# A four-layer graph network: layer 2 in written order, and inverse roots by ScalarE and a Newton step

## The chip, the cores and the metric

The kernel runs on one core of a Trainium2 chip. Its engines work side by side, each through its own queue of instructions: TensorE (PE in the profile, with its weight loads as PEld), VectorE (DVE), ScalarE (ACT), GpSimd (POOL) and SyncE (SP), which issues most DMAs. The metric is the device time of one execution in microseconds (us). One execution was also recorded by the hardware profiler; lines such as L941 are lines of the kernel before.

## The reference

16 graphs ("batches") share one adjacency matrix of 1024 x 1024; every node has 64 features. Four layers follow one another, each of them `x = layernorm(x + layer(x, adj))`:

```python
def gat(x, W, a, adj):                      # layers 0 and 2
    Wh = x @ W
    e = leaky_relu((Wh @ a1)[:, :, None] + (Wh @ a2)[:, None, :], 0.2)
    att = softmax(where(adj > 0, e, -big), axis=2)
    return elu(att @ Wh)

def softmax_average(x, w0, b0, wa, ba, adj):  # layer 1
    feat = softplus(x * w0 / sqrt(2) + b0)
    logits = where(adj > 0, feat * wa + ba, -big)   # one weight per feature
    return sum_j softmax_j(logits) * feat_j

def layer_3(x, adj, Wh, Wo, ...):             # four heads, then one output head
    z = leaky_relu(concat(attention(h, h, adj | eye) for each head), 0.2)
    return layernorm(leaky_relu(attention(z @ Wo, z @ Wo, adj | eye), 0.2)) * gamma + beta

def layernorm(x):
    return (x - mean(x)) / sqrt(var(x) + 1e-5)
```

`a1` and `a2` are the halves of `a`. The layer norm needs one inverse root of `var + eps` for each of 16 x 1024 nodes in every layer. How that inverse root is computed is half of the change.

## The kernel before

Everything stays in on-chip memory between the layers. The nodes are cut into C = 8 chunks of 128 partitions, and x lies in four tiles `xg[g]` of four batches each. `fast_path` (L579) is the program that runs; a general path is there for inputs that the fast path's flags reject.

**Layers 0 and 2** are one function, `gat_layer` (L862), called twice. A pair of batches is prepared in a chain: `prep_x` transposes x by PE into PSUM and ACT copies it to `xT` (L880, L881); `prep_s` makes the scores (PE `ps`, L886); `prep_top` copies them on DVE (`l_s`, L894), takes the maximum (L896) and gives it to GpSimd for a maximum over the partitions (`gtop`, L898); `prep_p` makes the factors `p` and `q` by two Exps on ACT (L909, L911); `prep_G` multiplies on PE (`pg`, L921) and takes an Exp on ACT (`G`, L922), in two halves; `prep_v` scales x by `p` on ACT (`vals`, L928).

Then each batch is eight units, one for a chunk of nodes. `unit(k)` is one DVE instruction over 128 x 1024, `e = max(G, q) * adjacency` (L941); `product(k, e)` two PE matmuls with `vals` as weights (`y`, L953), two units later (LAG = 2). In layer 0 PE also makes the row sums by separate matmuls (`u`, L964); in layer 2 a column of ones in `vals` gives them (`zero_mean`). When a batch's units are through, its tail runs in these steps: `evict` (ACT copies y, L971), `project` (PE, L983 and L987), `divide` (DVE L996 to L1001, ACT Exp `m` L1008), `residual` (DVE L1013, L1014), `norm` (DVE `bn_stats` L1021, and for every second batch `moments`), `shift` (DVE `bn_shift`) and `store` (ACT `scaled`, eight activations that write x).

The steps are put in slots (t, k): batch number and unit number. `slots` holds the list, and the loop over t and k calls a unit, a product and the slot's steps in turn. In both layers this is the order of the program; the order on each engine is however chosen by a planner that reorders instructions by cost and priority, since the loop doesn't run in a manual schedule. Layer 3 does: it is under `tc.manual_schedule(engines=in_order)`, in which PE, ACT, DVE and GpSimd keep the order as written.

**The inverse root.** `moments` (L733) works on a pair of batches (128 x 16 values) in layers 0 and 2 and on a group of four batches (128 x 32) in layer 1. DVE combines the statistics (L739 to L745), GpSimd raises the variance to the power −0.5 and DVE makes the shift from the result when the returned function is called:

```python
nc.gpsimd.tensor_tensor(t["rstd"], t["var"], neg_half[:, :n], ALU.pow)
def finish():
    v.scalar_tensor_tensor(t["shift"], t["mean"], -0.5, t["rstd"], ALU.mult, ALU.mult)
    return t["rstd"], t["shift"]
```

ACT's `scaled` (L758) then applies root and shift. Layer 3 already has another way (L718 to L726): ACT takes a Ln and an Exp with scale −0.5, and DVE one Newton step. Only its last batches use the power (L712, "late"). `most_var` keeps the largest variance seen, which one of the flags at the end is made from (L714). A list `soon` holds tasks that are called at the next `catch_up()`, in layer 3 alone.

**Layer 1** goes through the four groups g. `prep_l1` prepares the next group (transposes L1462, softplus by ACT's Abs, Exp, Relu and Ln L1464 to L1468, exponents L1476 to L1481, transposes L1490, split in two halves L1492 and L1493) while `product_l1` (L1507, 16 matmuls per chunk) and `average` (DVE L1516 to L1522) work on this one. The group's `shift` and four `rows` (eight activations each) are done beside the next group, and those of the last group in layer 2's first slots. In the same way the last steps of layer 0 run in layer 1 and those of layer 2 in layer 3 (`ending`).

Of the kernel before, what the change touches and what calls it, by code (L numbers as in the profile page):

```python
# [578 lines left out]
def fast_path(  # L579
# [66 lines left out]
    nc.vector.memset(ones, 1.0)  # L646
    neg_half = const.tile([P, GB * C], F32, tag="neg_half", name="neg_half")
    nc.vector.memset(neg_half, -0.5)
    most_var = const.tile([P, C], F32, tag="most_var", name="most_var")
    nc.vector.memset(most_var, 0.0)  # L650
# [14 lines left out]

    rings = {}
    soon = []

    def two_banks(name):
# [15 lines left out]
    def bc_mid(ap, n):  # L685

        return ap.unsqueeze(1).to_broadcast([P, n, ap.shape[1]])

    def normalizing(y, sq, late):

        n, t = y.shape[1], {}

        def mean():
            st = small.tile([P, n], F32, tag="ln_sum", name="ln_sum")
            nc.vector.tensor_reduce(st, y, AX.X, ALU.add)
            t["mean"] = small.tile([P, n], F32, tag="ln_mean", name="ln_mean")
            nc.vector.tensor_scalar(t["mean"], st, 1.0 / D, None, ALU.mult)

        def centre():
            nc.vector.tensor_tensor(y, y, bc_last(t["mean"], D), ALU.subtract)
            nc.vector.tensor_tensor(sq, y, y, ALU.mult)

        def scale():
            vs = small.tile([P, n], F32, tag="ln_vs", name="ln_vs")
            nc.vector.tensor_reduce(vs, sq, AX.X, ALU.add)
            ve = small.tile([P, n], F32, tag="ln_ve", name="ln_ve")
            nc.vector.tensor_scalar(ve, vs, 1.0 / D, LN_EPS, ALU.mult, ALU.add)
            rstd = small.tile([P, n], F32, tag="ln_rstd", name="ln_rstd")  # L710
            if late:
                nc.gpsimd.tensor_tensor(rstd, ve, neg_half[:, :n], ALU.pow)  # L712
                return rstd
            nc.vector.tensor_tensor(most_var[:, :n], most_var[:, :n], ve, ALU.max)  # L714


            def first():
                nc.scalar.activation(rstd, ve, AF.Ln)  # L718
                nc.scalar.activation(rstd, rstd, AF.Exp, scale=-0.5)
                soon.append(step)  # L720

            def step():
                t = small.tile([P, n], F32, tag="ln_step", name="ln_step", bufs=1)
                nc.vector.scalar_tensor_tensor(t, rstd, -0.5, rstd, ALU.mult, ALU.mult)
                nc.vector.tensor_tensor(t, t, ve, ALU.mult)
                nc.vector.scalar_tensor_tensor(rstd, t, 1.5, rstd, ALU.add, ALU.mult)  # L726

            soon.append(first)
            return rstd

        return mean, centre, scale

    def moments(st):  # L733


        n = st.shape[1]
        t = {k: small.tile([P, n], F32, tag=f"bn_{k}", name=f"bn_{k}") for k in ("mean", "d", "var", "rstd", "shift")}
        v = nc.vector
# [6 lines left out]
        v.tensor_tensor(t["var"], t["var"], t["d"], ALU.add)  # L745
        nc.gpsimd.tensor_tensor(t["rstd"], t["var"], neg_half[:, :n], ALU.pow)  # L746

        def finish():
            v.scalar_tensor_tensor(t["shift"], t["mean"], -0.5, t["rstd"], ALU.mult, ALU.mult)  # L749
            return t["rstd"], t["shift"]  # L750

        return finish

# [107 lines left out]

    def gat_layer(w, name, zero_mean, extra, first, own):  # L862

        w1, w4, ind, s12, sums, w_out = (w[k] for k in ("w1", "w4", "ind", "s12", "sums", "out"))
        F = D - 1 if zero_mean else D
# [68 lines left out]
        def attention(b):  # L936
# [73 lines left out]
            def residual():  # L1010

                v, m = held["v"], held["m"]
                nc.vector.scalar_tensor_tensor(v, v, 0.0, xb(b), ALU.max, ALU.add)  # L1013
                nc.vector.scalar_tensor_tensor(m, m, 1.0, v, ALU.min, ALU.add)  # L1014
            def norm():
                pair = stats.setdefault(b // 2, {})
# [5 lines left out]
                if b % 2:  # L1022
                    pair["end"] = moments(st)

            def shift():
                if b % 2:
                    stats[b // 2]["n"] = stats[b // 2]["end"]()

# [3 lines left out]

            return unit, product, [evict, project, divide, residual, norm, shift, store]

# [9 lines left out]
        for b in range(B):  # L1044
            end = (3, 6) if b % 2 == 0 else (3, 2)
            for task, (t, k) in zip(work[b][2], ((1, 1), (1, 2), (1, 4), (1, 6), (1, 7), (2, 1), end)):
                at(b + t, k, task)
# [12 lines left out]
        for (t, k), todo in extra.items():  # L1060
            for task in todo:
                at(t, k, task)
        first(ahead)
        for t in range(B + 1):
            for k in range(C):
                if t < B:
                    unit, product, _ = work[t]
# [4 lines left out]
                if t < B or (t == B and k < own):  # L1072
                    for task in slots.get((t, k), []):
                        task()

        return [task for t in range(B, B + 3) for k in range(C) for task in slots.get((t, k), []) if (t, k) >= (B, own)]
# [75 lines left out]
    def shift_of(key, sq):  # L1152
# [17 lines left out]

        if "s" in rings:
            soon.append(below)
        else:
            below()

# [236 lines left out]
    with tc.tile_pool(name="ps_g", bufs=1, space=bass.MemoryType.PSUM, reuse_waits="tile") as ps_g, tc.tile_pool(  # L1412
# [18 lines left out]
        extra = {(0, 6): [lambda: gat_setup(later["w2"], "l2", True)], (1, 6): [lambda: later["w3"]()]}  # L1431
        ending = gat_layer(w_0, "l0", False, extra, first, 3)

# [13 lines left out]
    with tc.tile_pool(name="l1", bufs=2, reuse_waits="tile") as l1, tc.tile_pool(  # L1447
# [66 lines left out]
        def average(g, ic, po, st):  # L1514
            r = l1.tile([P, 2, P], F32, tag="r1", name="r1")
            nc.vector.reciprocal(r, po[:, :, 1, :])  # L1516
# [11 lines left out]
        for g in range(NG):  # L1528
# [9 lines left out]

            def shift(mo=mo, end=moments(st)):
                mo["n"] = end()  # L1540
# [3 lines left out]

            last = [shift] + [lambda c=c, rows=rows: rows(c) for c in range(C * GB // 8)]

# [65 lines left out]
    with tc.tile_pool(name="ps_g", bufs=1, space=bass.MemoryType.PSUM, reuse_waits="tile") as ps_g, tc.tile_pool(  # L1612
# [3 lines left out]
        extra = {p: [task] for p, task in zip(places, ahead)}  # L1616
        for p, task in zip(((0, 1), (0, 3), (0, 7), (1, 3), (1, 7)), last):
            extra.setdefault(p, []).append(task)
# [4 lines left out]

        ending = gat_layer(later["w2"], "l2", True, extra, first, 5)
    for p, task in zip((2, 4, 8, 10, 13), ending):
        at(0, p, task)
# [13 lines left out]

    def catch_up():
        for task in [soon.pop(0) for _ in range(len(soon))]:
            task()

    def tasks(where, b, j):
# [10 lines left out]
    last = [(E, LAST + p, unit) for p, unit in enumerate(outs[E][1][0])]  # L1656


    in_order = {getattr(mybir.EngineType, e) for e in ("PE", "Activation", "DVE", "Pool")}

# [99 lines left out]
```

## Time and profile before

| | |
|---|---|
| Runs | 2199.07, 2201.24 and 2202.79 us; median 2201.24 |
| Profiled execution | 2202.97 us |
| Its span (first to last instruction) | 2201.1 us |
| Mean clock of TensorE, as a share of full speed | 0.971 |
| ACT busy | 1223.3 us (56%) |
| Stretches of the trace | layer 0 from 34 us, layer 1's first product at 337, layer 2's first unit at 514, layer 3 from 754 to the end |

The span leaves out what lies around the first and last instruction, 1.9 us here. A group in the profile names the line, the engine, the operation and its tiles (output <- inputs) with their shapes; "x20 | 71.9, 3596" means 20 instructions, 71.9 us busy, 3596 ns each on average; what follows is the idle time just before them and what ended most of it. A wait is written as "engine tile line <- engine tile line": who waited for whom, with the total in us, the count and the longest. Waits overlap with work on other engines, so they can't be summed over engines.

### The profile page before, as it was taken

To read this page: it belongs to the slowest core of one execution; us is meant where nothing else is said; L and a number is where in the kernel's file an instruction comes from. 1 tells how busy PE (TensorE), PEld (TensorE's weight loads), DVE (VectorE), ACT (ScalarE), POOL (GpSimd) and SP (SyncE) were. 2 spreads that over 40 slices of the span, in tenths; PEclk is the share of its full clock that TensorE was granted. 3 is DMA by queue.
4 is the path that set the end of the run, shared out by engine and by line. 5 is a ranking of instruction groups with operands and counts; after the bars stand their busy time and mean duration, and the time that the engine had idled before them with its cause. 6 is when DMAs were issued, how large, how long until landed. Compare 5 with 4: busy or idle time off the path is not lost.

```text
span 2201.1 us, 26623 instructions
## 1 busy us (share of the span) xinstructions
PE 2061.3 (94%) x10321; PEld 871.2 (40%) x10321; DVE 1835.6 (83%) x3141; ACT 1223.3 (56%) x1925; POOL 125.5 (6%) x97
## 2 busy tenths in 40 slices
PE   7999979897889899999999999999999999999993
PEld 3333337673334333433333333333333333333331
DVE  5877877886878886788889888889889889888997
ACT  4444544735544566655655665655665665565551
POOL 0010110011110100000000000000000000000001
PEclk9999989997999899999999999999999999999996
DMA  6000000000000010000000000000000000000000
GB/s 160 1 1 1 1 1 1 1 1 1 1 1 1 29 48 1 1 1 6 1 6 1 6 6 1 6 6 1 6 1 6 6 1 6 6 1 6 1 5 16
DMA packets 23655, 18.92 MB, mean 9 GB/s; under 512 B 19361, under 2 KB 19426, under 8 KB 23522
## 3 DMA queue, kind: packets, MB, share of 16 engines
q1 hardware_dynamic: 23218, 17.11, 2.7%
q8 instruction: 83, 1.36, 0.3%
q14 instruction: 50, 0.41, 0.1%
q10 hardware_dynamic: 304, 0.03, 0.0%
HBM read 12.95 MB, written 4.19 MB: 8 GB/s over the span
## 4 chain that ended last, share of the span: by engine, by line
PE 74%; DVE 18%; ACT 3%; POOL 2%; issue 1%; DMA 0%; SPq 0%; POOLq 0%; DVEq 0%; ACTq 0%
PE y L1235 18%; PE s L1223 17%; PE y_l L953 9%; PE s L1320 5%; PE y L1347 4%; DVE e L1228 4%; PE u_l L964 3%; DVE e L941 3%; PE po L1507 3%; PE po L1252 3%; POOL bn_rstd L746 2%; PE pg L921 2%; ACT e L1227 1%; PE ps L886 1%; PE po L987 1%
## 5 line engine op out<-in xcount | busy, mean ns | idle before, releaser
L1227 ACT ACTIVATE e<-s,shift 128x1024 f32<-128x1024 f32 x512 | 543.1, 1112 | 244.8 <-PE s L1223 239.2
L1228 DVE TENSOR_TENSOR e<-e,aT 128x1024 f32<-128x1024 f32 x512 | 602.6, 1220 | 86.8 <-ACT e L1227 84.7
L1223 PE MATMUL s<-hT 64*128 64x512 f32 x2048 | 509.9, 612 | 14.5 <-DVE top L1161 7.6
L1235 PE MATMUL y<-e,vals 128*64 128x512 f32 x2048 | 490.6, 601 | 3.4 <-ACT yT L1242 1.6
L941 DVE SCALAR_TENSOR_TENSOR e<-G_l,q,aT 128x1024 f32<-128x1024 f32 x256 | 319.0, 1273 | 11.2 <-ACT G_l L922 4.2
L953 PE MATMUL y_l<-e,vals_l 128*64 128x512 f32 x1024 | 273.4, 631 | 20.8 <-DVE e L941 20.7
L1223 PEld LDWEIGHTS s<-hT 64*128 64x128 f32 x2048 | 182.6, 186 | 254.7 <-issue 170.2
L1235 PEld LDWEIGHTS y<-e,vals 128*64 128x64 f32 x2048 | 131.0, 136 | 330.7 <-issue 258.8
L1325 ACT ACTIVATE e<-s,shift 128x1024 f32<-128x1024 f32 x128 | 142.1, 1113 | 85.5 <-PE s L1320 75.8
L1327 DVE TENSOR_TENSOR me<-e,aT 128x1024 f32<-128x1024 f32 x128 | 155.9, 1220 | 17.3 <-ACT e L1325 17.0
L1338 DVE SCALAR_TENSOR_TENSOR junk<-e,aN 128x1024 bf16<-128x1024 f32 x128 | 155.9, 1218 | 0.2
L1347 PE MATMUL y<-me,h2v 128*64 128x512 f32 x512 | 135.0, 608 | 10.0 <-DVE me L1327 9.8
L1320 PE MATMUL s<-h2T 64*128 64x512 f32 x512 | 137.4, 617 | 4.5 <-DVE h2v L1307 4.4
L953 PEld LDWEIGHTS y_l<-e,vals_l 128*64 128x64 f32 x1024 | 62.6, 139 | 167.0 <-issue 75.3
L1507 PE MATMUL po<-hi,aR 128*128 128x512 f32 x256 | 105.3, 411 | 13.1 <-DVE r L1517 11.9
L758 ACT ACTIVATE x<-m,bn_shift,bn_rstd 128x64 f32<-128x64 f32 x256 | 90.6, 430 | 32.2 <-DVE bn_shift L749 32.2
L1163 POOL PARTITION_ALL_REDUCE gtop<-top x48 | 28.1, 589 | 1355.5 <-DVE top L1161 852.1
L1507 PE MATMUL po<-lo,aR 128*128 128x512 f32 x256 | 103.3, 404 | 0.0
L746 POOL TENSOR_TENSOR bn_rstd<-bn_var,neg_half 128x16 f32<-128x16 f32 (+1 forms) x20 | 71.9, 3596 | 329.4 <-DVE bn_var L745 166.6
L964 PE MATMUL u_l<-e,only 128*32 128x512 f32 x512 | 78.7, 612 | 0.0
L1282 ACT COPY zT<-pzT 128x1024 f32<-128x1024 f32 x32 | 32.4, 1012 | 78.4 <-PE pzT L1281 78.4
L1252 PEld LDWEIGHTS po<-wb,yT 128*128 128x128 f32 x512 | 62.0, 190 | 34.0 <-issue 21.1
(209 smaller groups left out, 2108.6 us busy)
## 6 DMA issues: line engine op xcount, KB each, us to landing
adj<-in_adj_dram SPq DMA_DIRECT2D x16, 512.0 KB, 4.6
x<-in_x_dram SPq DMA_DIRECT2D x16, 256.0 KB, 5.1
out_dram<-res SPq DMA_DIRECT2D x16, 256.0 KB, 2.0
wl<-in_L_gnn_Wh_dram SPq DMA_DIRECT2D x2, 64.0 KB, 3.2
wo<-in_L_gnn_Wo_dram SPq DMA_DIRECT2D x1, 64.0 KB, 2.8
l_wd<-in_L_gnn_W_dram ACTq DMA_DIRECT2D x2, 16.0 KB, 3.9
l_wd<-in_L_gnn_W_dram SPq DMA_DIRECT2D x2, 16.0 KB, 2.0
bo<-in_L_gnn_bo_dram SPq DMA_DIRECT2D x1, 32.0 KB, 3.0
```

The lines of the kernel that those rows point to most:

```text
L941: nc.vector.scalar_tensor_tensor(e, G[b - b % 2][:, b % 2, :], pq[b - b % 2][1][:, k, b % 2 : b % 2 + 1], aT[:, k, :], ALU.max, ALU.mult,)
L953: nc.tensor.matmul(held["y"][h * D : (h + 1) * D, :], vals[b][:, k, :], e[:, h * HALF : (h + 1) * HALF], start=(k == 0), stop=(k == C - 1),)
L964: nc.tensor.matmul(held["t"][r * 32 : (r + 1) * 32, :], only[b][:, kk, :], ee[:, h * HALF : (h + 1) * HALF], start=(kk < 2), stop=(kk >= C ...
L1223: nc.tensor.matmul(s[:, i, :], hT[rows, k * P : (k + 1) * P], hT[rows, cols], start=True, stop=True)
L1227: nc.scalar.activation(e, s, AF.Exp, bias=shifts[b, n])
L1228: nc.vector.tensor_tensor(e, e, bc_mid(aT[:, k, cols], 2), ALU.mult)
L1235: nc.tensor.matmul(held[h][i * D : (i + 1) * D, :], vals[b][:, k, :], e[:, i, :], start=(k == 0), stop=(k == C - 1),)
L1320: nc.tensor.matmul(s[:, i, :], hT[rows, (i + k // CH) % 2, k % CH * P : (k % CH + 1) * P], hT[rows, 0, :], start=True, stop=True,)
L1327: nc.vector.tensor_tensor(m, e, aT[:, k, :].rearrange("p (i q) -> p i q", i=2), ALU.mult)
L1338: nc.vector.scalar_tensor_tensor(junk, held.pop(k).rearrange("p i q -> p (i q)"), 1.0, aN[:, k, :], ALU.mult, ALU.mult, accum_out=sums[:, ...
L1347: nc.tensor.matmul(held["o"][h * D : (h + 1) * D, :], vals["out", b][:, k, :], e[:, h, :], start=(k == 0), stop=(k == C - 1),)
L1507: nc.tensor.matmul(po.rearrange("p q k f -> p (q k f)"), aR[:, k, ic * P : (ic + 1) * P], e[:, k].rearrange("p q k f -> p (q k f)"), start ...
```

## The change

Two things are changed together, and steps are moved for them.

First, `moments` no longer asks GpSimd. A helper `inverse_root` holds what layer 3 had in place: it notes the largest variance, and returns `root` (Ln and Exp on ACT) and `step` (three DVE instructions). `moments` returns `root` and `finish`; `finish` does the step and then the shift. The power stays in layer 3's late batches alone, so `neg_half` shrinks and `most_var` grows.

```diff
+    def inverse_root(r, ve):
+        n = ve.shape[1]
+        nc.vector.tensor_tensor(most_var[:, :n], most_var[:, :n], ve, ALU.max)
+
+        def root():
+            nc.scalar.activation(r, ve, AF.Ln)
+            nc.scalar.activation(r, r, AF.Exp, scale=-0.5)
+
+        def step():
+            t = small.tile([P, n], F32, tag="ln_step", name="ln_step", bufs=1)
+            nc.vector.scalar_tensor_tensor(t, r, -0.5, r, ALU.mult, ALU.mult)
+            nc.vector.tensor_tensor(t, t, ve, ALU.mult)
+            nc.vector.scalar_tensor_tensor(r, t, 1.5, r, ALU.add, ALU.mult)
+
+        return root, step
...
-        nc.gpsimd.tensor_tensor(t["rstd"], t["var"], neg_half[:, :n], ALU.pow)
+        root, step = inverse_root(t["rstd"], t["var"])
 
         def finish():
+            step()
             v.scalar_tensor_tensor(t["shift"], t["mean"], -0.5, t["rstd"], ALU.mult, ALU.mult)
             return t["rstd"], t["shift"]
 
-        return finish
+        return root, finish
```

Second, the loop of layer 2 (not its preparation ahead of the loop, and not layer 0) runs in a manual schedule: PE, ACT, DVE and GpSimd then execute what the loop issues in the order as written.

```diff
-    def gat_layer(w, name, zero_mean, extra, first, own):
+    def gat_layer(w, name, zero_mean, extra, first, own, ordered):
+        run = ExitStack()
...
+            def root():
+                if b % 2:
+                    stats[b // 2]["end"][0]()
+
             def shift():
                 if b % 2:
-                    stats[b // 2]["n"] = stats[b // 2]["end"]()
+                    stats[b // 2]["n"] = stats[b // 2]["end"][1]()
...
-            return unit, product, [evict, project, divide, residual, norm, shift, store]
+            return unit, product, [evict, project, divide, residual, norm, root, shift, store]
...
-            for task, (t, k) in zip(work[b][2], ((1, 1), (1, 2), (1, 4), (1, 6), (1, 7), (2, 1), end)):
+            for task, (t, k) in zip(work[b][2], ((1, 1), (1, 3), (1, 4), (1, 6), (1, 7), (2, 0), (2, 2), end)):
                 at(b + t, k, task)
...
         first(ahead)
+        if ordered:
+            run.enter_context(tc.manual_schedule(engines=in_order))
         for t in range(B + 1):
             for k in range(C):
+                catch_up()
                 if t < B:
                     unit, product, _ = work[t]
                     e = unit(k)
...
+        run.close()
```

In the slots, `project` moves from unit 2 to unit 3 of the next batch, `root` gets (2, 0), and `shift` goes from (2, 1) to (2, 2). This holds for both layers. `catch_up` is now there from the start and is called at each unit; the second half of layer 3's `shift_of` (`below`) always goes through `soon`, also for the first ones, which are issued in layer 2's last batch.

The steps of layer 1's last group in layer 2 are six and begin one unit earlier; layer 2's ending is six steps in place of five. A scratch tile of `average` has one buffer instead of two.

```diff
-            r = l1.tile([P, 2, P], F32, tag="r1", name="r1")
+            r = l1.tile([P, 2, P], F32, tag="r1", name="r1", bufs=1)
...
-            last = [shift] + [lambda c=c, rows=rows: rows(c) for c in range(C * GB // 8)]
+            last = [root, shift] + [lambda c=c, rows=rows: rows(c) for c in range(C * GB // 8)]
...
-        for p, task in zip(((0, 1), (0, 3), (0, 7), (1, 3), (1, 7)), last):
+        for p, task in zip(((0, 0), (0, 1), (0, 3), (0, 7), (1, 3), (1, 7)), last):
             extra.setdefault(p, []).append(task)
...
-        ending = gat_layer(later["w2"], "l2", True, extra, first, 5)
-    for p, task in zip((2, 4, 8, 10, 13), ending):
+        ending = gat_layer(later["w2"], "l2", True, extra, first, 5, True)
+    for p, task in zip((1, 4, 7, 10, 14, 16), ending):
         at(0, p, task)
```

Layer 0's call ends in `False`, so its order stays the planner's.

More of the change, by code (lines that the diff above doesn't have):

```diff
@@ L646, in fast_path @@
     nc.vector.memset(ones, 1.0)
-    neg_half = const.tile([P, GB * C], F32, tag="neg_half", name="neg_half")
+    neg_half = const.tile([P, C], F32, tag="neg_half", name="neg_half")
     nc.vector.memset(neg_half, -0.5)
-    most_var = const.tile([P, C], F32, tag="most_var", name="most_var")
+    most_var = const.tile([P, GB * C], F32, tag="most_var", name="most_var")
     nc.vector.memset(most_var, 0.0)
@@ L667, in fast_path, with catch_up @@
     soon = []
+    in_order = {getattr(mybir.EngineType, e) for e in ("PE", "Activation", "DVE", "Pool")}
+    def catch_up():
+        for task in [soon.pop(0) for _ in range(len(soon))]:
+            task()
     def two_banks(name):
@@ L711, in scale @@
             if late:
-                nc.gpsimd.tensor_tensor(rstd, ve, neg_half[:, :n], ALU.pow)
+                nc.gpsimd.tensor_tensor(rstd, ve, neg_half, ALU.pow)
                 return rstd
-            nc.vector.tensor_tensor(most_var[:, :n], most_var[:, :n], ve, ALU.max)
+            root, step = inverse_root(rstd, ve)
             def first():
-                nc.scalar.activation(rstd, ve, AF.Ln)
-                nc.scalar.activation(rstd, rstd, AF.Exp, scale=-0.5)
+                root()
                 soon.append(step)
[L722 to L726, printed above, removed]
             soon.append(first)
@@ L1168, in below @@
             nc.vector.tensor_scalar(sh, gtop, -1.0, HEADROOM, ALU.mult, ALU.add)
[L1171 to L1174, printed above, removed]
+        soon.append(below)
     def prep_x(b):
@@ L1431, in fast_path @@
         extra = {(0, 6): [lambda: gat_setup(later["w2"], "l2", True)], (1, 6): [lambda: later["w3"]()]}
-        ending = gat_layer(w_0, "l0", False, extra, first, 3)
+        ending = gat_layer(w_0, "l0", False, extra, first, 3, False)
     w0 = row_bc(L1_w0.rearrange("a b -> (a b)"), 1, "w0")
@@ L1537, in fast_path, with shift @@
             mo = {}
-            def shift(mo=mo, end=moments(st)):
+            root, finish = moments(st)
+            def shift(mo=mo, end=finish):
                 mo["n"] = end()
@@ L1639, in fast_path @@
     aN = l3.tile([P, C, N], BF16, tag="aN", name="aN", bufs=1)
-    def catch_up():
-        for task in [soon.pop(0) for _ in range(len(soon))]:
-            task()
     def tasks(where, b, j):
@@ L1656, in fast_path @@
     last = [(E, LAST + p, unit) for p, unit in enumerate(outs[E][1][0])]
-    in_order = {getattr(mybir.EngineType, e) for e in ("PE", "Activation", "DVE", "Pool")}
     def run(queue):
```

## The prediction

> **What bounds the kernel now.** I read the engine totals first, then the cost groups, then a table of the span cut at the layers, then the waits and timelines of the worst stretches.
>
> ```profile
> PE 2061.3 (94%) x10321; PEld 871.2 (40%) x10321; DVE 1835.6 (83%) x3141; ACT 1223.3 (56%) x1925; POOL 125.5 (6%) x97
> ...
> L746 POOL TENSOR_TENSOR bn_rstd<-bn_var,neg_half 128x16 f32<-128x16 f32 (+1 forms) x20 | 71.9, 3596 | 329.4 <-DVE bn_var L745 166.6
> ```
>
> PE's 94% would leave little to win, and the pow (L746) totals only 72 us. But 94% is an average over stages with different limits. The next view has, for each stretch: window, length, busy PE, PEld, DVE, ACT, POOL, then PE clock.
>
> ```profile
> 34.00:306.00 272.00, 271.79 (x1609) 95.27 (x1609) 215.26 (x436) 122.01 (x342) 29.75 (x14) 0.99 0.05 8
> 306.00:337.00 31.00, 14.56 (x90) 12.19 (x89) 21.12 (x47) 19.86 (x28) 2.90 (x1) 0.61 0.00 1
> 337.00:495.00 158.00, 143.86 (x678) 116.75 (x676) 132.19 (x301) 79.18 (x146) 16.54 (x4) 0.96 0.00 1
> 495.00:514.00 19.00, 8.09 (x29) 5.42 (x28) 1.16 (x9) 11.56 (x34) 6.05 (x3) 0.50 0.00 1
> 514.00:754.00 240.00, 214.47 (x1080) 89.97 (x1082) 204.24 (x403) 116.38 (x335) 28.96 (x13) 0.93 0.01 2
> ```
>
> Layer 0 (34 to 306) keeps PE busy all the time: its pows cost nothing now. Layer 1 (337 to 495), the crossing to layer 2 (495 to 514) and layer 2 (514 to 754) have holes on every engine. Layer 3, from 754, is not touched except for its first tasks. DVE's waits from 494 to 764 (total us, times, longest) say what the holes are:
>
> ```profile
> DVE bn_shift L749 <- POOL bn_rstd L746: 27.8, 8, 5.6
> DVE l_s L894 <- PE ps L886: 21.3, 7, 8.0
> DVE e L941 <- ACT G_l L922: 4.2, 1, 4.2
> ```
>
> So in and before layer 2 DVE is the scarce engine, and it stands still for 53 us, half of it for GpSimd.
>
> **Layer 2 itself.** Three windows that each hold one pair of batches, same columns:
>
> ```profile
> 562.40:594.60 32.20, 29.46 (x144) 12.33 (x144) 26.31 (x56) 15.84 (x45) 4.24 (x2) 0.89 0.01 1
> 658.80:689.60 30.80, 26.64 (x144) 11.59 (x144) 26.30 (x56) 15.22 (x44) 4.17 (x2) 1.00 0.00 1
> 689.60:720.20 30.60, 28.23 (x144) 11.89 (x144) 26.26 (x56) 15.32 (x44) 4.17 (x2) 0.94 0.00 1
> ```
>
> Each has 26.3 us of DVE work in a period of 30.6 to 32.2. PE's busy figure includes its own waiting matmuls, so I take PE's need from layer 0, where it never waits: 272/8 = 34.0 us per pair, less the `u` products that layer 2 lacks (L964, 78.7 us over 8 pairs = 9.8), gives 24.2. DVE is the limit, with stalls on top. From the first unit (514.13) to the last (753.35) DVE is idle 35.6 of 239.2 us: 22.1 for the pow, 13.3 for the `l_s` copy.
>
> *The pow.* POOL's timeline (start, duration; in brackets the idle time before and its releaser):
>
> ```profile
> 550.82 1.31 POOL L898 PARTITION_ALL_REDUCE gtop<-top  x1 [41.17 <-DVE top L896]
> 559.38 2.95 POOL L746 TENSOR_TENSOR bn_rstd<-bn_var,neg_half 128x16 f32<-128x16 f32 x1 [7.25 <-DVE e L941]
> ```
>
> `bn_var` (L745) was ready at 556.60, yet the pow starts 2.78 us later, 7.25 after the all-reduce. By the row's duration alone the change saves 2.95 per root. The Trainium skill, "GPSIMD Engine Reference", section 2.1 "Instruction dispatch", says the first call of a freshly loaded GpSimd routine pays about 6 us with no instruction to show for it, and here an all-reduce and a pow alternate. By that rule the delay from `bn_var` to result is 2.95 plus whatever of the reload isn't hidden: 5.73 here, of which DVE covers two units (2.48) and stalls 3.37. The trace sides with the rule, and I count stalls, not durations: 22.1 us in seven waits.
>
> *The `l_s` wait* (about 2.2 per pair) is an order effect: the planner put the copy on DVE ahead of units that were ready, before PE had got to `ps` (L886). In written order `prep_s` and `prep_top` are a slot apart (1.3 us of units on DVE) and the copy follows the slot's unit, so most of it goes.
>
> *What is added.* Per pair: one DVE max and three Newton steps. Layer 3's rows L724 and L725 last 0.16 each and such small operations follow one another 0.1 apart: 4 × 0.1 = 0.4 (0.7 if each counts fully). On ACT a Ln and an Exp, 0.21 each (L718, L719), for which two slots are left before the step; ACT has 15 of 31 us filled. A rule speaks against this pair: the Trainium skill, "ScalarE: Activation LUTs", section "What ACT_TABLE_LOAD costs", asks 2.66 us for every switch of table set; 20 roots with two switches each would be an estimated 106 us of ACT, more than the whole gain. The trace answers:
>
> ```profile
> L719 ACT ACTIVATE ln_rstd<-ln_rstd x28: 208/208/209, 952.1 to 2130.4; 128x8 f32<-128x8 f32 x28
> ...
> L640 ACT ACT_TABLE_LOAD  x1: 1283/1283/1283, 0.7 to 0.7; - x1
> ```
>
> Layer 3 already alternates Ln and Exp 28 times with one load in the whole program. I take 0.
>
> *The written order as a risk.* Each engine now executes strictly in program order, so a late instruction holds all behind it. No trace of before shows this for layer 2; I walked one pair through with the durations above. Moved `project` (slot 3 instead of 2) leaves about 0.5 us until `divide` in slot 4; behind that copy (L996) on DVE queue the next units, and behind those PE's products. `residual` in slot 6 waits for ACT's Exp (L1008), which may stand behind `G`'s second half; about 1 us of slack. Everything else has over a unit. Bounds: no stall at all, or 2 us per batch, as much as the planner's `l_s` waits now. I take 0.6 us per pair, 5 in all, nearer the low end because the walk found no negative slack.
>
> Sum of layer 2: idle 35.6 goes, stalls of 5 and 3.5 of DVE work come: −27. With PE's 24.2 below DVE's 26.7 plus 0.6, the period becomes about 27.3.
>
> **Crossing from layer 1 to layer 2.** ACT, then DVE:
>
> ```profile
> 500.58 4.08 ACT L758 ACTIVATE x<-x,bn_shift,bn_rstd 128x64 f32<-128x64 f32 x12 [9.01 <-DVE bn_shift L749]
> 504.58 1.04 ACT L881 COPY xT_l<-pxT 128x512 f32<-128x512 f32 x2
> ...
> 508.80 0.19 DVE L894 COPY l_s<-ps 128x32 f32<-128x32 f32 x1 [7.95 <-PE ps L886]
> ...
> 514.13 15.63 DVE L941 SCALAR_TENSOR_TENSOR e<-G_l,q,aT 128x1024 f32<-128x1024 f32 x13 [4.23 <-ACT G_l L922]
> ```
>
> The last pow of layer 1 ends at 500.32. Only then do `bn_shift` (DVE), the twelve scalings (ACT) and the two `xT` copies *behind* those scalings run; `ps`, `l_s`, the maximum, `p`, `G` follow in a chain. Group 3 doesn't feed the first pair; it only stands ahead of it. Afterwards `root`, `shift` and `rows` come at (0,0) and later, behind the first pair's preparation: `l_s` about 494.8, `gtop` 496.4, `p`/`q` 497, the halves of `G` 499 and 501 to 502 (pg at half clock, as now: 0.50). First unit at 502 instead of 514.1: −12. The 32 scalings move into the first slots; 32 × 0.34 = 10.9 us of ACT lie beside the first pair, and could cost 2 us once (in the 5 above).
>
> **Layer 1.** At three group boundaries a 128x32 pow of 5.48 us stops DVE 5.3 each and PE about 4 each (`r` L1517). The replacement is a Ln, an Exp and three small DVE steps, but the softplus chain on ACT is then what DVE meets first, about 1.7 us. Net −3.2, −3.2 and, without such preparation behind it, −4: −10. **Start of layer 1:** a `bn_shift` wait of 3.04 sits ahead of the exponents: −2. **Start of layer 3:** 10.15 us from the last unit to L1228 (763.50); without the pow for the tail: −3.5. **Layer 0:** DVE has 7 us of cover per pair, PE bounds: 0 (with that cover gone, 8 × 0.4 = 3 more).
>
> **Sum.** −27 −12 −10 −2 −3.5 = −54.5. Profiled execution 2202.97 − 54.5 = 2148.5; it was 1.7 above the runs' median of 2201.24, so **2147**.
>
> **Rivals.**
>
> 1. *The forecast*, DVE-bound layer 2 at 27.3 per pair: 2147, own range 2135 to 2158. Chance 0.55.
> 2. *PE takes over layer 2.* For: 24.2 us is only 2.5 below DVE, and the clock was 0.89 in one of the windows; 24.2 × 0.99/0.89 = 26.9, and head-of-line waits come on top: period 29, 8 × 1.7 = 13 lost: 2160. Against: the 1.00 window. Chance 0.2.
> 3. *The order costs half the gain*: 2 us of stalls per batch in layer 2 instead of 0.3 (+27): 2174. Or layer 1 gives nothing, its wait merely passing to the softplus chain (+10), and part of this. For: slacks of 0.5 and 1 us. Chance 0.15.
> 4. *Slower.* In strict order `G`'s second half (ACT) waits for `pg`, which waits behind `project` on PE, and ACT's Exp for `divide` stands behind it; `residual` then stops DVE, `e` stops, PE starves, every batch. To cancel 54.5 it must cost 3.4 us per batch; at 4 us: 2147 + 16 × 4 − 5 = 2206. For: the longest such ACT wait now is 6 us. Against: the slack by slots. Chance 0.04.
> 5. *It doesn't do what it says*: `l_s` still waits on PE in written order, so only the pows and the crossing are won: 2147 + 13 = 2160. Chance 0.06.
>
> Changes within 0.2% (4.4 us) can't be told from none: faster 0.94, same 0.02, slower 0.04. The range 2128 to 2174 takes in rivals 2 and 5, most of 3, and more gain downward if stalls vanish (−5), layer 1 yields its full 16 (−6) and the clock helps.
>
> **What would show it.** POOL keeps only all-reduces and the late pows, with no 6 us gap. Layer 2's DVE idle falls from 35.6 to under 10, pairs at 27 to 28; the first unit comes about 8 us after layer 1's end, not 19; layer 0 is still 272. If DVE waits for `ps` or `po`, rivals 2 or 5 hold; if for `m` or `G`, 3 or 4. A second table load or a longer layer 0 would make the sum wrong from the start.

## The result and the profile after

The changed kernel takes 2163.77 us (median of 4 runs, 2161.82 to 2170.64) against 2202.01 for the kernel before (4 runs, 2199.07 to 2203.13). The ratio is 0.9834 with a 95% interval of 0.981 to 0.9858: a gain of 31 to 42 us, where 54.5 had been forecast. The profiled execution took 2170.64 us with a span of 2168.8. It is the slowest of the four, so its stages sum to a gain of 32.3 us, 6 less than the medians show: differences of stages below are those of single executions, and good to a few us.

Line numbers of the changed kernel differ: the unit is L959 (was L941), `y` L971 (L953), the copy of the sums in `divide` L1014 (L996), `l_s` L912 (L894). The page's first part, and the table by stage (columns as before):

```profile
PE 2047.2 (94%) x10321; PEld 866.2 (40%) x10321; DVE 1852.5 (85%) x3221; ACT 1227.5 (57%) x1965; POOL 51.0 (2%) x77
```

```profile
34.00:288.00 254.00, 254.00 (x1582) 92.80 (x1583) 209.40 (x451) 113.51 (x326) 4.37 (x7) 0.98 0.04 7
288.00:317.00 29.00, 15.98 (x101) 11.13 (x98) 23.22 (x58) 21.84 (x36) 0.00 (x0) 0.76 0.00 1
317.00:457.00 140.00, 136.15 (x664) 111.29 (x662) 132.82 (x303) 83.39 (x161) 0.00 (x0) 1.00 0.00 1
457.00:468.00 11.00, 7.65 (x32) 4.13 (x32) 4.69 (x19) 6.28 (x19) 0.35 (x1) 0.72 0.00 0
468.00:725.00 257.00, 228.24 (x1120) 99.95 (x1120) 219.56 (x459) 124.98 (x367) 8.99 (x8) 0.83 0.01 3
```

The roots are off GpSimd: between 288 and 457 it runs nothing. Layer 1 and the crossing are shorter, as forecast. But the stretch with layer 0, where next to nothing was to happen, is 19 us shorter, and layer 2, which was to bring half the gain, got longer. By the events that bound the stages:

| Stage | before | after | difference | forecast |
|---|---|---|---|---|
| start to layer 1's first product | 335.9 | 316.7 | −19.2 | −2 |
| layer 1, first to last product | 154.2 | 139.5 | −14.7 | −10 |
| last product to layer 2's first unit | 24.0 | 11.5 | −12.5 | −12 |
| layer 2, first to last unit | 239.3 | 256.7 | +17.4 | −27 |
| last unit to layer 3's first | 10.1 | 6.9 | −3.2 | −3.5 |
| layer 3 | 1437.6 | 1437.5 | 0 | 0 |

DVE's waits from layer 2's first unit to its last:

```profile
DVE l_sums L1014 <- PE po L1005: 27.4, 11, 4.0
DVE e L959 <- ACT G_l L940: 5.5, 1, 5.5
DVE v L1031 <- ACT m L1026: 2.5, 2, 1.7
DVE top L1188 <- PE pn L1184: 2.3, 1, 2.3
DVE l_s L912 <- PE ps L904: 1.7, 2, 1.2
```

The waits for the power (22.1 us) are gone, those for `ps` (13.3) nearly, and 27.4 us of waits for `po` have come: `divide` waits for `project`. (The 5.5 is the gap before the first unit and lies in the crossing.) DVE's busy time rose too, from 203.6 to 219.2 between the first and the last unit. With the roots alone it is 206.9, as the experiments show.

**Where layer 2 waits.** PE and then DVE of the changed kernel, at the largest of these waits:

```profile
591.41 0.66 PE L898 MATMUL pxT<-ident,x 128*128 128x128 f32 x4
592.70 1.08 PE L971 MATMUL y_l<-e,vals_l 128*64 128x512 f32 x4 [0.63 <-ACT xT_l L899]
593.71 2.41 PE L904 MATMUL ps<-l_w,xT_l 128*128 128x4 f32 x16
596.05 1.98 PE L971 MATMUL y_l<-e,vals_l 128*64 128x512 f32 x4
597.96 1.87 PE L1001 MATMUL po<-l_ind,yT_l 128*128 128x2 f32 x8
599.75 1.98 PE L1005 MATMUL po<-l_wo,yT_l 64*128 64x64 f32 x16
```

```profile
601.76 0.17 DVE L1014 TENSOR_SCALAR l_sums<-po 128x8 f32<-128x8 f32 x1 [4.01 <-PE po L1005]
```

In even batches `prep_x`, `prep_s` and `project` of two different batches stand in slots 0 to 3 together, beside the products, and `divide` in slot 4 needs the last of them. PE comes late, and DVE, which must keep its order, can't go on to the next units. Six of the eleven waits, 18.0 us, are of this kind. The other five, 9.4 us, come in odd batches, where the two halves of `pg` stand in slots 2 and 3 beside `project`.

The durations tell a second thing: from 595 to 605 the granted clock is 0.50 (`y` x4 takes 1.98 instead of 1.08, `project` 3.7 instead of 2.0). The half clock isn't needed for a wait, though. The first one follows 9 us at full clock:

```profile
479.00:488.00 9.00, 9.00 (x56) 3.93 (x55) 6.95 (x9) 2.10 (x4) 0.00 (x0) 1.00 0.00 0
...
487.88 0.17 DVE L1014 TENSOR_SCALAR l_sums<-po 128x8 f32<-128x8 f32 x1 [2.05 <-PE po L1005]
```

**Where layer 0 won.** The 19.2 us have three parts. The first unit comes at 29.9 us instead of 33.9; it waits for the adjacency (`aT`), and in the other eleven kernels' executions it comes anywhere from 29.1 to 32.9, so these 4.0 us can't be put down to the change. From the first unit to the last `u`, layer 0 itself takes 262.8 us instead of 273.3, 10.5 less. From there to layer 1's first product it is 24.0 instead of 28.7. The layer first: a stretch of PE in the kernel before, then one of the changed kernel.

```profile
145.87 1.05 PE L964 MATMUL u_l<-e,only 128*32 128x512 f32 x2
146.84 1.95 PE L886 MATMUL ps<-l_w,xT_l 128*128 128x4 f32 x16
148.72 1.06 PE L964 MATMUL u_l<-e,only 128*32 128x512 f32 x6
...
159.31 1.12 PE L921 MATMUL pg<-xT_l,l_w 64*128 64x512 f32 x2
160.36 1.05 PE L983 MATMUL po<-l_ind,ysum_l 128*128 128x2 f32 x8
161.35 1.11 PE L987 MATMUL po<-l_wd,yT_l 64*128 64x64 f32 x16
162.30 1.07 PE L921 MATMUL pg<-xT_l,l_w 64*128 64x512 f32 x2
```

```profile
146.08 1.07 PE L982 MATMUL u_l<-e,only 128*32 128x512 f32 x8
...
153.81 1.13 PE L939 MATMUL pg<-xT_l,l_w 64*128 64x512 f32 x4
```

Eight records of `u` (four matmuls on four different quarters of the columns) take 1.0 us together, but two of them take 0.97 and the other six 0.99 when `ps` stands between. `pg` likewise: two matmuls on different halves of the rows take 1.06 together and 1.05 plus about 1.0 apart. The matmuls of such a group run side by side, as the Trainium skill, "TensorE: Matmul & The Clock Gate", section "Part 3: Packing small matmuls — row/col tiling", says of matmuls at different tile positions; a foreign one between them takes that away. The planner had broken nine of the 64 groups of `u` before and breaks two now, and of `pg` five of 14 in the loop before and none now. PE's busy time from the first unit to the last `u`, for `u` and for `pg`, before and then changed (window, length, busy PE, clock, DMA):

```profile
33.90:307.30 273.40, 78.67 (x512) 0.99 0.05 8
33.90:307.30 273.40, 21.26 (x56) 0.99 0.05 8
```

```profile
29.90:292.70 262.80, 72.01 (x512) 0.98 0.06 11
29.90:292.70 262.80, 15.47 (x56) 0.98 0.06 11
```

That is 12.5 us less, a little more than the layer lost: the changed kernel ran at half clock from 31.8 to 42.1, 10.3 us, the kernel before for 3.4 us of the layer.

### The profile page after: what moved, and what is told of

Read it like the earlier page. It is cut to its first block, busy times and chain, and to the rows that moved or that the text cites. A ratio compares the mean times of both kernels' runs of the same rounds, so it can differ in the third digit from the quotient of the medians.

```text
span 2168.8 us, 26641 instructions
## 1 busy us (share of the span) xinstructions
PE 2047.2 (94%) x10321; PEld 866.2 (40%) x10321; DVE 1852.5 (85%) x3221; ACT 1227.5 (57%) x1965; POOL 51.0 (2%) x77
## 4 chain that ended last, share of the span: by engine, by line
PE 73%; DVE 21%; ACT 4%; issue 1%; DMA 0%; POOL 0%; SPq 0%; POOLq 0%; DVEq 0%; ACTq 0%
PE y L1259 18%; PE s L1247 17%; PE y_l L971 8%; PE s L1344 5%; PE y L1371 4%; DVE e L1252 4%; PE u_l L982 3%; DVE e L959 3%; PE po L1276 3%; PE po L1531 3%; PE po L1005 2%; PE pg L939 2%; PE po L1001 1%; PE ps L904 1%; ACT e L1251 1%
## 5 line engine op out<-in xcount | busy, mean ns | idle before, releaser
L959 DVE SCALAR_TENSOR_TENSOR e<-G_l,q,aT 128x1024 f32<-128x1024 f32 x256 | 319.9, 1276 | 20.5 <-ACT G_l L940 12.4
L971 PE MATMUL y_l<-e,vals_l 128*64 128x512 f32 x1024 | 278.8, 660 | 27.9 <-DVE e L959 26.3
L1351 DVE TENSOR_TENSOR me<-e,aT 128x1024 f32<-128x1024 f32 x128 | 155.8, 1220 | 16.8 <-ACT e L1349 16.5
L1371 PE MATMUL y<-me,h2v 128*64 128x512 f32 x512 | 135.3, 609 | 10.5 <-DVE me L1351 10.4
L971 PEld LDWEIGHTS y_l<-e,vals_l 128*64 128x64 f32 x1024 | 65.3, 146 | 184.9 <-issue 75.4
L1276 PE MATMUL po<-wb,yT 128*128 128x130 f32 x512 | 73.8, 287 | 1.3 <-ACT e L1251 1.2
L982 PE MATMUL u_l<-e,only 128*32 128x512 f32 x512 | 72.0, 612 | 0.0
L1344 PEld LDWEIGHTS s<-h2T 64*128 64x128 f32 x512 | 46.6, 186 | 63.7 <-issue 41.4
```

Of the source, the lines that this page charges most:

```text
L959: nc.vector.scalar_tensor_tensor(e, G[b - b % 2][:, b % 2, :], pq[b - b % 2][1][:, k, b % 2 : b % 2 + 1], aT[:, k, :], ALU.max, ALU.mult,)
L971: nc.tensor.matmul(held["y"][h * D : (h + 1) * D, :], vals[b][:, k, :], e[:, h * HALF : (h + 1) * HALF], start=(k == 0), stop=(k == C - 1),)
L1276: nc.tensor.matmul(o[:, j // 2, j % 2, :], held["y"][:, c * P : (c + 1) * P], wb[:, n, :], start=True, stop=True,)
L1344: nc.tensor.matmul(s[:, i, :], hT[rows, (i + k // CH) % 2, k % CH * P : (k % CH + 1) * P], hT[rows, 0, :], start=True, stop=True,)
L1351: nc.vector.tensor_tensor(m, e, aT[:, k, :].rearrange("p (i q) -> p i q", i=2), ALU.mult)
L1371: nc.tensor.matmul(held["o"][h * D : (h + 1) * D, :], vals["out", b][:, k, :], e[:, h, :], start=(k == 0), stop=(k == C - 1),)
```

## The experiments

Two theories of layer 2 stood against each other. A: the written order loses what the roots win, because it makes DVE wait for `project`. B: the roots' longer chain on DVE loses it. For layer 0 the question was which edit had made the planner keep the groups whole. All but the third kernel are the changed kernel with an edit; the third is the kernel before with one. The diffs show the lines that matter; where a step moves past the end of layer 2's loop, the loop is one unit longer (`first, 6`).

**The roots, without the written order in layer 2**

```diff
-        ending = gat_layer(later["w2"], "l2", True, extra, first, 5, True)
+        ending = gat_layer(later["w2"], "l2", True, extra, first, 5, False)
```

> The roots as in the changed kernel, but layer 2's order left to the planner. Theory A, the written order is what layer 2 lost by (it took 257 us from first to last unit, 240.5 before): here layer 2 takes 225 to 232 us, 240.5 less 22 of waits for the power plus some 8 of new DVE work, and the whole 2133 to 2142. Theory B, the longer root chain on DVE is what it lost by: layer 2 stays at 250 or more, the whole at 2158 or more. Layer 0 about 254 from 34 us on in both.

**The written order, without the roots**

```diff
-        root, step = inverse_root(t["rstd"], t["var"])
+        def root():
+            nc.gpsimd.tensor_tensor(t["rstd"], t["var"], neg_half[:, :n], ALU.pow)
         def finish():
-            step()
```

> The written order and all moved slots, but GpSimd's power for every root, issued in the slot of `root`. Theory A: layer 2 is as slow as in the changed kernel or slower (257 to 285, the power's waits on top). Theory B: layer 2 is at most 240. Layer 0 tells which part gave it 17 us: about 254 if the moved slots did (the planner then keeps PE's u and pg groups whole), about 272 if the power's absence did.

**The slot of `project` alone, in the kernel before**

```diff
-  zip(work[b][2], ((1, 1), (1, 2), (1, 4), (1, 6), (1, 7), (2, 1), end))
+  zip(work[b][2], ((1, 1), (1, 3), (1, 4), (1, 6), (1, 7), (2, 1), end))
```

> The kernel before with one edit: project in slot 3 instead of slot 2, in layers 0 and 2. If that slot is what keeps PE's u and pg groups whole in layer 0, layer 0 is some 17 us shorter and the whole about 2185; if not, within 5 us of 2202.

**`divide` one slot later in layer 2**

```diff
-  ((1, 1), (1, 3), (1, 4), (1, 6), (1, 7), (2, 0), (2, 2), end)
+  ((1, 1), (1, 3), (1, 5), (1, 7), (2, 0), (2, 1), (2, 3), end)   # layer 2 only
```

> The changed kernel with layer 2's divide one slot later, two behind project, and the steps after it moved on by one. Theory A1, DVE waits for po (27 us) only because divide stands one slot behind project while PE is behind: the wait falls under 8 us, layer 2 to 232 to 238, the whole to about 2143. Theory A2, PE has too much to do in layer 2 at the clock it gets (0.83): the wait only changes its name, layer 2 stays at 250 or more, the whole at 2158 or more.

What these four gave; the stages are from each one's profiled execution (layer 0 from its first unit to its last `u`), the ratio is to the kernel before in runs on the same chip:

| Kernel | median us | ratio (95%) | layer 0 | layer 1's first product | layer 1 | crossing | layer 2 | DVE waits for `po` in layer 2 | clock in layer 2 |
|---|---|---|---|---|---|---|---|---|---|
| before | 2202.01 | | 273.3 | 335.9 | 154.2 | 24.0 | 239.3 | 0.2 | 0.94 |
| changed | 2163.77 | 0.9834 (0.981–0.9858) | 262.8 | 316.7 | 139.5 | 11.5 | 256.7 | 27.4 | 0.83 |
| roots only | 2143.39 | 0.9744 (0.9722–0.9766) | 259.6 | 314.5 | 141.6 | 12.8 | 223.6 | 7.9 | 0.93 |
| order only | 2190.27 | 0.9944 (0.9927–0.9961) | 259.4 | 313.4 | 161.3 | 21.6 | 250.5 | 24.6 | 0.85 |
| slot 3 only | 2193.78 | 0.9981 (0.9967–0.9996) | 259.5 | 313.4 | 155.0 | 24.1 | 252.2 | 28.3 | 0.87 |
| divide later | 2152.66 | 0.978 (0.9764–0.9797) | 259.1 | 314.0 | 141.6 | 12.3 | 236.9 | 6.5 | 0.88 |

Theory A holds in the main and B falls: with the roots and the planner's order layer 2 takes 223.6 us, a little under the 225 to 232 that A expected, and the whole is 20 us faster than with both parts of the change (by the medians; 29 by the profiled executions). Its row in the table by stage:

```profile
468.90:692.50 223.60, 216.55 (x1093) 97.29 (x1093) 206.94 (x434) 120.66 (x359) 8.13 (x7) 0.93 0.01 2
```

DVE is busy 206.9 us there, 3.3 more than before: that is the price of the roots.

The second kernel fits neither expectation. With the power in written order layer 2 takes 250.5 us, between B's 240 and A's 257. The waits for `po` are there (24.6 us), as A has it, but the waits for the power, 22.1 us before, are down to 2.4. GpSimd's rows show why:

```profile
563.24 1.30 POOL L916 PARTITION_ALL_REDUCE gtop<-top  x1 [17.61 <-DVE top L914]
575.97 3.83 POOL L763 TENSOR_TENSOR bn_rstd<-bn_var,neg_half 128x16 f32<-128x16 f32 x1 [11.44 <-DVE bn_var L761]
```

In the kernel before, the six powers of layer 2 that follow an all-reduce start 6.9 to 7.4 us after its end, 2.4 to 2.9 us after `bn_var` was ready: the delay that the prediction took for a reload. Here they are asked for 9 to 12 us after the all-reduce and start within 0.2 us of `bn_var`. So in written order the delay lies in the pause between the two, `shift` comes one unit later, and layer 2 gains nothing from the roots (256.7 with them). In these runs they pay there only under the planner: with `project` in slot 3 they bring 252.2 down to 223.6. The power kept, but with the all-reduce or the scores moved, is a rival to the roots in layer 2 that was not run.

The stages also say what the roots bring elsewhere: layer 1 and the crossing are short in every kernel with them (139 to 142, 11 to 13) and long in every kernel without (154 to 161, 22 to 24).

Layer 0 belongs to neither the roots nor the order. One digit, the slot of `project`, in the kernel before gives all of it (273.3 to 259.5), with 62 whole groups of `u` and two broken, and 3.9 us between layer 0's last `u` and layer 1's first product as well. Why the planner keeps the groups whole with this digit was not looked into. The same digit costs layer 2 13 us (239.3 to 252.2): `project` has moved closer to `divide`, and DVE waits 28.3 us for `po` under the planner's order as well. So the expected 2185 was missed by 9: the edit nearly cancels itself. The written order with `project` left in slot 2 was not run, so how much of the 27.4 us comes from the order and how much from this slot stays open.

`divide` later takes 20 of the 33 us that separate the changed kernel's layer 2 from that of roots only. That supports A1, though the whole missed its 2143 by 10. The layer still is 13 us longer, and DVE's waits in it sum to no more than in roots only (16.8 and 16.4 us): the rest is DVE's busy time, 217.1 against 206.9.

**The scores later: is it crowding on PE?**

```diff
+            late = 3 if ordered else 0
-            chain += [(lambda b=b: prep_s(b), -2, 2), (lambda b=b: prep_top(b), -2, 3)]
+            chain += [(lambda b=b: prep_s(b), -2, 2 + late), (lambda b=b: prep_top(b), -2, 3 + late)]
```

> The changed kernel with prep_s and prep_top of layer 2 in slots 5 and 6 instead of 2 and 3. Theory A1 (PE is crowded in slots 0 to 3 of every second batch by pxT, ps and project, so project is late for divide): DVE's wait for po falls from 27 us to under 12 and layer 2 from 257 to 235 to 243. Rival, the wait comes from the half clock alone and not from the crowding: the wait stays over 20, layer 2 over 250.

**Four idle matmuls where PE pauses: is it the clock?**

```diff
+                if ordered and t < B and (k in (0, 1) if t % 2 == 0 else k in (6, 7)):
+                    for i in range(4):
+                        nc.tensor.matmul(rings["w"][:, i * P : (i + 1) * P], ident, ident, start=True, stop=True)
```

> The changed kernel with four idle matmuls of 128x128 on PE in slots 0 and 1 of even and 6 and 7 of odd batches of layer 2, where PE pauses: 0.6 us each time, 2.4 per pair, 19 in the layer. Theory D (the pauses bring the half clock, and the half clock makes project late): the clock in layer 2 rises from 0.83 to over 0.92 and the layer gets shorter, 240 to 252, though PE has more to do. Rival, the clock follows from the waits and doesn't make them: the layer gets longer, 257 to 276.

**`project` in slot 2 in layer 2 alone, with the roots and the planner's order**

```diff
-  ((1, 1), (1, 3), (1, 4), ...)
+  ((1, 1), (1, 2 if zero_mean else 3), (1, 4), ...)
```

> The roots by ScalarE, layer 2 left to the planner, and project in slot 3 in layer 0 but slot 2 in layer 2. With the power, slot 3 cost layer 2 13 us (252.2 against 239.3). If that holds with the new roots too, layer 2 takes 208 to 215 us instead of 223.6 and the whole 2128 to 2135; if the planner's order with the new roots hides it, layer 2 is within 4 us of 223.6 and the whole within 4 of 2143.

**`divide` later, and dependent DVE steps one per slot**

```diff
+    def in_turn(*ops):
+        ops[0]()
+        if not apart[0]:
+            for op in ops[1:]:
+                op()
+        elif ops[1:]:
+            soon.append(lambda: in_turn(*ops[1:]))
...
-            step()
-            v.scalar_tensor_tensor(t["shift"], t["mean"], -0.5, t["rstd"], ALU.mult, ALU.mult)
+            in_turn(
+                lambda: v.scalar_tensor_tensor(s, r, -0.5, r, ALU.mult, ALU.mult),
+                lambda: v.tensor_tensor(s, s, ve, ALU.mult),
+                lambda: v.scalar_tensor_tensor(r, s, 1.5, r, ALU.add, ALU.mult),
+                lambda: v.scalar_tensor_tensor(t["shift"], t["mean"], -0.5, r, ALU.mult, ALU.mult),
+            )
```

The steps of `divide`, `residual`, the moments and `prep_top` are split in the same way, and `residual`, `norm`, `root`, `shift` and `store` come later by what that takes.

> divide_late with the short dependent DVE steps of layer 2 (divide, residual, moments, Newton step, the scores' copy and maximum) issued one per slot, a unit between each two, and norm, root, shift and store later by what that takes. Theory C, about 1 us per pair of DVE time in the written order is an instruction waiting for the one just before it, and as much again the chain of the new root: DVE busy in layer 2 falls from 217 to 205 to 210 us, layer 2 from 237 to 223 to 230. Rival, DVE isn't what bounds layer 2 any more: layer 2 stays within 4 us of 237.

| Kernel | median us | ratio (95%) | layer 2 | DVE busy in it | DVE waits for `po` | clock in layer 2 |
|---|---|---|---|---|---|---|
| scores later | 2151.2 | 0.9788 (0.9761–0.9815) | 229.7 | 218.3 | 5.3 | 0.95 |
| PE filled | 2177.94 | 0.9897 (0.9867–0.9927) | 263.3 | 220.0 | 19.8 | 0.94 |
| slot 2 in layer 2 | 2141.64 | 0.9732 (0.9704–0.9761) | 224.8 | 206.6 | 2.2 | 0.92 |
| divide later, steps apart | 2142.66 | 0.9747 (0.972–0.9774) | 227.1 | 212.5 | 4.0 | 0.86 |

Taking the scores out of the crowd brings layer 2 from 256.7 to 229.7, even below what was expected. The waits for `po` in even batches fall from 18.0 to 0.6 us; in odd ones, where the scores never stood, 4.7 of 9.4 are left. The clock comes back by itself, to 0.95. The whole gains less than the stage, 13 us by the medians: the changed kernel's profiled execution was the slowest of its four, this one the fastest. In its table row PE is busy 199.5 us instead of 227.6 with the same instructions:

```profile
468.80:698.40 229.60, 199.52 (x1116) 85.57 (x1116) 218.32 (x454) 124.73 (x367) 9.00 (x8) 0.95 0.01 2
```

PE filled is the counterpart. The clock rises to 0.94 as theory D has it, and the layer gets 6.6 us longer all the same. The longest wait for `po` falls from 4.0 to 1.8 us, but 15.0 us of waits for `ps` appear, because the filling stands in the crowded slots. The filling adds to the crowding, so this run alone doesn't weigh the two; together with the wait at full clock above and the scores later it does. Crowding makes the delay, and the half clock adds to the worst of it: at 601.76 above, the four rows at half clock cost an estimated 3 of the 4.0 us, by the same rows' durations at full clock. The clock alone isn't the cause. Filling the pauses raised the clock, but what brings the half clock stays open: PE's pauses in layer 2 sum to 30.1 us in the changed kernel (clock 0.83) and to 31.1 with the scores later (0.95).

With the roots, the slot of `project` in layer 2 no longer matters under the planner's order (224.8 and 223.6); the 13 us that it cost with the power had been expected to come off and didn't.

The steps apart remove most of that last part. Two stretches of DVE, the root's chain in the changed kernel, and the moments of the kernel before, in which such small instructions are independent or have a unit between them:

```profile
581.13 0.16 DVE L707 SCALAR_TENSOR_TENSOR ln_step<-bn_rstd 128x16 f32<-128x16 f32 x1
581.33 0.18 DVE L708 TENSOR_TENSOR ln_step<-ln_step,bn_var 128x16 f32<-128x16 f32 x1
581.54 0.17 DVE L709 SCALAR_TENSOR_TENSOR bn_rstd<-ln_step,bn_rstd 128x16 f32<-128x16 f32 x1
581.75 0.17 DVE L766 SCALAR_TENSOR_TENSOR bn_shift<-bn_mean,bn_rstd 128x16 f32<-128x16 f32 x1
581.84 2.47 DVE L959 SCALAR_TENSOR_TENSOR e<-G_l,q,aT 128x1024 f32<-128x1024 f32 x2
```

```profile
682.34 0.18 DVE L741 TENSOR_TENSOR bn_mean<-bn 128x16 f32<-128x16 f32 x1
682.44 0.17 DVE L743 SCALAR_TENSOR_TENSOR bn_d<-bn_d 128x16 f32<-128x16 f32 x1
682.52 0.17 DVE L744 TENSOR_SCALAR bn_var<-bn_var 128x16 f32<-128x16 f32 x1
682.60 1.27 DVE L941 SCALAR_TENSOR_TENSOR e<-G_l,q,aT 128x1024 f32<-128x1024 f32 x1
683.80 0.17 DVE L745 TENSOR_TENSOR bn_var<-bn_var,bn_d 128x16 f32<-128x16 f32 x1
```

In these rows a small instruction that reads the result of the one just before it starts 0.20 or 0.21 us after that one's start; one that doesn't, 0.08 to 0.10 us. The planner puts a unit between (L941 before L745); the written order had them back to back. Apart, DVE is busy 4.6 us less, which is less than expected (212.5 against 205 to 210), and layer 2 is 9.8 us shorter than with `divide` later alone (236.9 to 227.1). The other half of that is waits, and may come from the later slots of the steps as much as from their distance.

**Both edits of the written order, and two more**

The first has late scores and steps apart, with `divide` in slot 4; the second late scores with layer 0 in written order too, the third the roots with late scores under the planner:

```diff
+            late = 4 if ordered else 0            # first: slots 6 and 7, p, G and vals one slot later; second: 3
...
-        ending = gat_layer(w_0, "l0", False, extra, first, 3, False)
+        ending = gat_layer(w_0, "l0", False, extra, first, 3, True)            # second
...
+            late = 3 if zero_mean else 0                                       # third
-        ending = gat_layer(later["w2"], "l2", True, extra, first, 5, True)
+        ending = gat_layer(later["w2"], "l2", True, extra, first, 5, False)    # third
```

> Layer 2 with both edits that helped by themselves: the scores after project (slots 6 and 7, and what follows from them one slot later) and the short dependent DVE steps one per slot. If the two losses of the written order are separate, they add up: DVE busy about 210 instead of 218, waits under 8, layer 2 at 217 to 222 us, the whole at 2132 to 2138. If one bound replaces the other (PE's clock, ACT), layer 2 stays at 227 or more, the whole at 2142 or more.

> The kernel with late scores, with layer 0's loop in written order too and its scores late as well. PE bounds layer 0, and in the written order no u or pg group is broken; broken groups are about 2 us of the 254 left. If only groups matter there, layer 0 takes 250 to 256 us and the whole 2146 to 2152. If the written order makes PE wait in layer 0 as in layer 2 (for e behind divide, or for the scores), layer 0 gets 262 or more and the whole 2158 or more.

> The roots by ScalarE, layer 2 left to the planner, but its scores in slots 5 and 6. If the crowding of PE in slots 0 to 3 costs the planner's order too (its DVE waits for po and m are 16 us), layer 2 takes 212 to 219 instead of 223.6, the whole 2130 to 2138. If the planner moves around it anyway, layer 2 is within 3 us of 223.6 and the whole within 4 of 2143.

| Kernel | median us | ratio (95%) | layer 1's first product | layer 2 | DVE busy in it | clock in layer 2 |
|---|---|---|---|---|---|---|
| scores later, steps apart | 2137.82 | 0.9717 (0.9679–0.9755) | 311.9 | 220.0 | 214.3 | 0.97 |
| layer 0 ordered too | 2148.66 | 0.9761 (0.9722–0.98) | 321.5 | 233.7 | 218.5 | 0.94 |
| roots, planner, scores later | 2136.23 | 0.9698 (0.9654–0.9741) | 315.4 | 220.3 | 206.5 | 0.93 |

The two edits add up: layer 2 at 220.0 us, within the expected 217 to 222 (DVE's busy time, 214.3, was expected at 210). With both edits the written order and, with late scores, the planner's are equal, in layer 2 (220.0 and 220.3) and as a whole, where the intervals overlap. The late scores bring the planner's layer 2 only 3.3 us, between the two expectations. By the ratios both kernels are 26 to 30 us under the changed kernel.

Written order in layer 0 brings nothing that can be told: the interval overlaps that of the scores later alone. All 64 groups of `u` are whole there, yet layer 0 takes 264.9 us from its first unit to its last `u`. The trace shows why: layer 0's first batches also prepare weights of later layers, and in written order PE stands still for these short chains, 3.3 us between 44 and 67 us. The longest of these pauses:

```profile
46.83 0.69 PE L868 MATMUL l_pw<-l_wd,l_less 128*128 128x64 f32 x2 [1.90 <-DVE l_less L863]
```

The clock is 0.50 from 46.7 to 50.1 and from 67.2 to 74.0, where it is full in all the other kernels. So PE's waits and the half clock took back more than the last two groups could give.

## Why the prediction was right, and where its sum was wrong

The direction and the range held; 2163.8 lies between the forecast (2147) and the case in which the order costs half the gain (2174). The gain was 38 us instead of 54.5, and the parts were further off than the sum. That the whole stayed in the range is in part luck: layer 2 missed its term by 44 us (−27 forecast, +17.4), and the start and layer 0 with what follows it gave 17 more than forecast, for a reason that no term had. Without these 17 the changed kernel would have taken some 2181, above the range.

- **The roots** were right outside layer 2. The whole program still has one table load, the power's stalls are gone, and the new work was put at 3.5 us and measured 3.3 (roots only). The crossing fits (−12 forecast, −12.5). Layer 1 gave 14.7 instead of 10: the 1.7 us that DVE was to wait for the softplus chain at each boundary is not in the trace; 4.6 us of waits for `po` and 0.3 others are all that is left there. In layer 2 the 22.1 us of waits for the power were counted as the roots' gain, but the order and the moved slots take 19.7 of them without the roots.
- **Layer 3's start** fits in number only (−3.5, −3.2). It was put down to the power's absence, but from layer 2's last unit to layer 3's first it takes 7.4 us with the power in written order and 9.7 with the roots and the planner (10.1 before): most of it came with the order and the moved slots.
- **"Layer 0: 0"** failed. The reading that PE bounds the layer and the power costs nothing there was right. It left out that the work of a PE that never waits depends on the order, and that moving `project` also gives the planner another order. The term was −10.5 in the changed kernel and −13.8 in slot 3 only. The −2 for layer 1's start measured −4.7, of which the slot alone gives 3.9.
- **"I take 0.6 us per pair, 5 in all"**, the stalls of the written order, is the step that failed in layer 2. It measured 27.4 us of waits for `project` alone. The walk had checked `project` to `divide` for one pair, with 0.5 us of slack, but had not added up what PE carries in slots 0 to 3 of an even batch, when the scores of the next pair stand before `project`. The bound of 2 us per batch, 32 in all, held it; the choice near the low end didn't. The price of waiting at half clock wasn't in the sum either.
- **The `l_s` wait** went, as forecast (13.3 to 1.7). In its place DVE waits for `po`.
- **DVE's new work in the written order**: 0.4 us per pair had been taken at the spacing of independent instructions. A chain of four takes 0.7 (581.13 to 581.84), and the order put the old steps back to back too; DVE's busy time rose by 15.6 us, of which the roots are 3.3 and some 2 belong to layer 3's first steps. The prediction's period and sum don't meet either: 27.3 us per pair makes 218 in eight, its sum 212, since the layer's ends hold less DVE work than the three windows in its middle.

Of the rivals, the third comes closest in size: the order was to cost 2 us of stalls per batch, and the 27.4 us are 1.7. But it looked for the stalls at ACT's `m` and `G`, which make 2.5 us in the layer, and its total of 2174 had no gain in layer 0. PE taking over layer 2 comes closest in words: DVE waits for `po`, and the clock did fall (0.94 to 0.83). But PE was late in certain slots, not overloaded: with the same instructions in other slots DVE bounds the layer and the clock is back at 0.95.

## What to carry to other kernels

A written order must be summed per slot and engine, over all the batches whose steps meet in the slot; slack per step of one batch isn't enough. Put a consumer several units behind its producer, and something independent between short dependent steps. When a change moves a step under a planner, look at what it does to groups of matmuls that run side by side, even in a stage where the step itself is hidden; and try the parts of a change alone, since here the changed kernel is 20 us slower than one with the roots only.

## What was unexpected of the hardware

- Four matmuls with 32 columns each took 1.0 us together and 1.96 in two pieces (0.97 and 0.99): breaking one group costs as much as the group.
- A pause of PE of 2.2 us (609.0 to 611.2 in the changed kernel) was followed by 3.5 us at half clock, and pauses of 0.44 and 0.63 us in 590 to 592.7 by ten, which is up to 5 us of work lost. But the same pauses with the scores later, 2.2 us at 597.5 and 0.44 and 0.63 in 610.8 to 613.5, were followed by full clock. A pause alone doesn't decide it. The two places of the changed kernel, then those with the scores later:

```profile
595.00:605.00 10.00, 10.00 (x42) 5.90 (x44) 5.86 (x10) 2.37 (x10) 1.24 (x1) 0.50 0.00 0
...
612.00:615.50 3.50, 3.50 (x10) 0.80 (x8) 3.40 (x10) 1.53 (x3) 0.00 (x0) 0.51 0.02 5
```

```profile
597.50:604.00 6.50, 4.32 (x24) 1.96 (x26) 6.33 (x18) 2.53 (x6) 0.00 (x0) 1.00 0.01 4
610.80:620.00 9.20, 8.12 (x53) 3.94 (x53) 9.13 (x19) 6.09 (x17) 0.00 (x0) 1.00 0.00 0
```
